# The tail of a GNN and mixture-of-experts layer: half of the experts' rows added on TensorE, small steps by pairs of loads, amplitude and base by diagonals

## The chip, the cores and the metric

The program runs on one core of a Trainium2 chip. The core has TensorE (PE, with its weight loads shown apart as PEld), VectorE (DVE), ScalarE (ACT), GpSimd (POOL) and SyncE (SP), which here only issues transfers, and 16 DMA engines. The metric is the device time of one execution in microseconds (us), given as the median of the runs.

## The reference, cut to what matters

A graph convolution with a residual, a top-2 mixture of 64 experts, a batch normalisation over the 12,500 nodes, then a sum with the input and a layer normalisation over the 256 columns. What the change touches is the end, from `y` on:

```python
    m = segment_sum(h[src], dst, n) * rsqrt(deg_in)[:, None]
    x = m @ W_gc + b_gc + (feats @ W_res + b_res)
    core = _moe_ff(x, Wg, bg, w1, b1, w2, b2)      # two experts a node, summed
    y = x + core
    mean = jnp.mean(y, axis=0)
    var = jnp.mean((y - mean) ** 2, axis=0)
    return (y - mean) * rsqrt(var + BN_EPS) * gamma + beta
...
x = _layernorm(x + gnn(x, ...), axis=-1)           # eps 1e-5
```

All of it is float32. Nodes are 12,500 rows, 256 columns.

## The kernel before

The program is one straight line of stages: the edges are ordered, the rows of the neighbours are gathered and summed on TensorE (the longest stage), the dense layers and the router follow, then the 64 experts, and last the tail, which begins at line 1400. A scheduler puts the instructions of each engine into an order when the program is built: by the order of the program, but an instruction that could start, by the scheduler's own reckoning, may go ahead of one that could not. On the chip each engine runs its list in that order. The SP list of transfers is such a list too: a transfer that waits for a buffer holds back those behind it.

The nodes are cut into 98 tiles of 128 (the last has 84), and the tail handles them in the 14 entries of `LOADS`: twelve of eight tiles (1 MB each), then tile 96 and tile 97 alone. The big buffer `acc` (`acc2` is its view in two halves of 128 columns) holds `x`, the residual stream, with nodes on the partitions; the experts have added their outputs to `z_d` in memory.

Pass 1 (L1417 to L1440) runs over `LOADS`. L1420 reads a load of `z_d` into `zt` (four buffers); L1422 adds it to `acc` on VectorE; L1433 turns each 128 x 128 block on TensorE with `ident`, four blocks to a PSUM buffer `q` of one bank (five buffers); L1438 takes the statistics of `q` on VectorE; L1440 copies `q` back over `acc` on ScalarE, so that columns are on the partitions afterwards. Then `fetch` (L1443 to L1447) reads the first five loads of the input `x` into the buffers `z` (pool `f_x`, five buffers).

Between the passes (L1452 to L1472) the statistics are merged and the two values per column, `amp` and `base`, are made. The helper `rsqrt` (L186 to L196) takes a square root on ScalarE, which has to load its table first, and four small steps on VectorE.

Pass 2 (L1473 to L1514) runs over `LOADS` again. L1478 scales each half of the load by `amp` and adds `base`, on ScalarE, in place. L1486 turns the blocks back on TensorE, four to a `q`; L1490 adds `q` to the input rows in `z` on VectorE; L1492 takes the statistics of each row. L1495 to L1508, with `rsqrt` among them, are the small steps, 13 on VectorE and a square root on ScalarE, over 8 columns at a time, which give each row's scale `rs` and shift `m`. L1510 applies them, one tile at a time, on ScalarE; L1513 stores the load, and L1514 fetches the load five further on into the buffer that this store frees.

Of the kernel before, what the change touches and what calls it, by code (L numbers as in the profile page):

```python
# [8 lines left out]
F32 = mybir.dt.float32  # L9
# [4 lines left out]
AF = mybir.ActivationFunctionType  # L14
ALU = mybir.AluOpType
# [4 lines left out]
P = 128  # L20
N = 12500
D = 256
# [3 lines left out]
EPS = 1e-5  # L26
# [70 lines left out]
LOADS = [(t, 8) for t in range(0, 96, 8)] + [(96, 1), (97, 1)]  # L97
# [4 lines left out]
def gnn_moe_kernel(  # L102
# [17 lines left out]
    nc = tc.nc  # L120
    V, S, T, GP = nc.vector, nc.scalar, nc.tensor, nc.gpsimd
# [10 lines left out]
    def rows(t):  # L132
        return P if t < NT - 1 else RAG
# [13 lines left out]
    ident = const.tile([P, P], F32)  # L147
# [7 lines left out]
    ones_f = const.tile([P, P], F32)  # L155
# [30 lines left out]
    def rsqrt(pool, o, d, tag=""):  # L186

        shape = [d.shape[0], d.shape[1]]
        r = pool.tile(shape, F32, name="rsq_r" + tag)
        S.activation(r, d, AF.Sqrt)  # L190
        V.reciprocal(r, r)
        q = pool.tile(shape, F32, name="rsq_q" + tag)
        V.tensor_mul(q, r, r)
        V.tensor_mul(q, q, d)
        V.tensor_scalar(q, q, -0.5, 1.5, op0=ALU.mult, op1=ALU.add)
        V.tensor_mul(o, r, q)  # L196
# [26 lines left out]
    acc2 = acc.rearrange("p (h n) -> p h n", h=2)  # L223
# [7 lines left out]
    bias = edge.tile([P, DL], F32)  # L231
# [21 lines left out]
    with ExitStack() as stack:  # L253
        one = stack.enter_context(tc.tile_pool(name="e_one", bufs=1))
        two = stack.enter_context(tc.tile_pool(name="e_two", bufs=2))
        ps1 = stack.enter_context(tc.tile_pool(name="e_ps1", bufs=1, space=PSUM))
        ps2 = stack.enter_context(tc.tile_pool(name="e_ps2", bufs=2, space=PSUM))
# [150 lines left out]
        for c0 in range(0, C0 + 1, CH):  # L408
            n = min(CH, C0 + 1 - c0)
# [143 lines left out]
    with ExitStack() as stack:  # L553
# [4 lines left out]
        for i, (t0, n) in enumerate(pieces):  # L558
            r = rows(t0)
# [74 lines left out]
    with ExitStack() as stack:  # L634
# [226 lines left out]
        def fetch(t0):  # L861
            if t0 >= NT:
                return
            n, r = (2, P) if t0 < NT - 2 else (1, rows(t0))
            xts[t0] = two.tile([P, 2, D], F32, name="xt", bufs=3)
            S.dma_start(xts[t0][:r, :n], x[t0 * P : t0 * P + (n - 1) * P + r].rearrange(
                "(t p) d -> p t d", p=r))
# [314 lines left out]
    with ExitStack() as stack:  # L1182
# [27 lines left out]
        at = 0  # L1210
# [189 lines left out]
    with ExitStack() as stack:  # L1400
        one = stack.enter_context(tc.tile_pool(name="f_one", bufs=1))
        two = stack.enter_context(tc.tile_pool(name="f_two", bufs=2))
        xq = stack.enter_context(tc.tile_pool(name="f_x", bufs=5))
        zq_stack = stack.enter_context(ExitStack())
        zq = zq_stack.enter_context(tc.tile_pool(name="f_z", bufs=4))
        ps1 = stack.enter_context(tc.tile_pool(name="f_ps1", bufs=1, space=PSUM))
        ps2 = stack.enter_context(tc.tile_pool(name="f_ps2", bufs=5, space=PSUM))

        gam = one.tile([P, 2], F32)
        nc.sync.dma_start(gam, gamma.rearrange("(h p) -> p h", p=P))  # L1410
        bet = one.tile([P, 2], F32)
        nc.sync.dma_start(bet, beta.rearrange("(h p) -> p h", p=P))


        stat = one.tile([P, 2, 25, 6], F32)
        z3 = z_d[:NP].rearrange("(t p) d -> p t d", p=P)
        for t0, n in LOADS:  # L1417
            r = rows(t0)
            zt = zq.tile([P, 8, D], F32, name="zt")
            nc.sync.dma_start(zt[:r, :n], z3[:r, t0 : t0 + n])  # L1420
            y = acc2[:r, :, t0 * P : (t0 + n) * P].rearrange("p h (t d) -> p t h d", d=P)
            V.tensor_add(y, y, zt[:r, :n].rearrange("p t (h d) -> p t h d", h=2))  # L1422
            if t0 == 96:
                continue
            for h in range(2):
                for b in range(0, n, 4) if t0 < 96 else [-1]:
                    q = ps2.tile([P, 4, P], F32, name="q")
                    at = 0
                    for i in range(4):
                        t = t0 + b + i  # L1430
                        if t < NT:
                            r = rows(t)
                            T.transpose(  # L1433
                                q[:, i, :r], acc2[:r, h, t * P : (t + 1) * P], ident[:r, :r]
                            )
                            at += r
                    q = q.rearrange("p a b -> p (a b)")[:, :at]
                    V.bn_stats(stat[:, h, (t0 + b) // 4], q)  # L1438

                    S.copy(acc2[:, h, (t0 + b) * P : (t0 + b) * P + at], q)  # L1440
        xt = {}

        def fetch(k):  # L1443
            if k < len(LOADS):
                t0, n = LOADS[k]
                xt[k] = xq.tile([P, 8, D], F32, name="z")
                nc.sync.dma_start(xt[k][: rows(t0), :n], part_of(x, t0, n))  # L1447

        for k in range(5):
            fetch(k)  # L1450

        mv = one.tile([P, 2, 2, 2], F32)  # L1452
        for h in range(2):
            V.bn_aggr(mv[:, h, 0], stat[:, h, :24])
            V.bn_aggr(mv[:, h, 1], stat[:, h, 24])

        full, rest = 24 * 512 / N, (N - 24 * 512) / N
        mean = one.tile([P, 2], F32)
        var = one.tile([P, 2], F32)
        gap = one.tile([P, 2], F32)  # L1460
        V.tensor_sub(gap, mv[:, :, 1, 0], mv[:, :, 0, 0])
        V.scalar_tensor_tensor(mean, gap, rest, mv[:, :, 0, 0], op0=ALU.mult, op1=ALU.add)
        V.tensor_mul(gap, gap, gap)
        V.tensor_scalar(var, mv[:, :, 0, 1], full, EPS, op0=ALU.mult, op1=ALU.add)
        V.scalar_tensor_tensor(var, mv[:, :, 1, 1], rest, var, op0=ALU.mult, op1=ALU.add)
        V.scalar_tensor_tensor(var, gap, full * rest, var, op0=ALU.mult, op1=ALU.add)
        amp = one.tile([P, 2], F32)
        rsqrt(one, amp, var, "_f")
        V.tensor_mul(amp, amp, gam)
        base = one.tile([P, 2], F32)  # L1470
        V.tensor_mul(base, mean, amp)
        V.tensor_sub(base, bet, base)  # L1472
        for g, (t0, n) in enumerate(LOADS):  # L1473
            r = rows(t0)
            z = xt[g][:r, :n]
            for h in range(2):
                y = acc2[:, h, t0 * P : (t0 + n - 1) * P + r]
                S.activation(y, y, AF.Identity, bias=base[:, h : h + 1], scale=amp[:, h : h + 1])  # L1478
            st = two.tile([P, 8, 6], F32, name="st")
            for i in range(0, n, 2):  # L1480
                k = min(2, n - i)
                q = ps2.tile([P, 4, P], F32, name="q")
                for j in range(k):
                    t = t0 + i + j
                    for h in range(2):
                        T.transpose(  # L1486
                            q[:r, 2 * j + h], acc2[:, h, t * P : t * P + r], ident
                        )
                zi = z[:, i : i + k].rearrange("p t d -> p (t d)")
                V.tensor_add(zi, q[:r, : 2 * k].rearrange("p a b -> p (a b)"), zi)  # L1490
                for j in range(k):
                    V.bn_stats(st[:r, i + j], z[:, i + j])  # L1492

            m = two.tile([P, 8], F32, name="m")
            V.tensor_add(m[:r, :n], st[:r, :n, 1], st[:r, :n, 4])  # L1495
            V.tensor_scalar_mul(m[:r, :n], m[:r, :n], -0.5)
            gap = two.tile([P, 8], F32, name="gap")
            V.tensor_sub(gap[:r, :n], st[:r, :n, 1], st[:r, :n, 4])
            V.tensor_mul(gap[:r, :n], gap[:r, :n], gap[:r, :n])
            ve = two.tile([P, 8], F32, name="ve")  # L1500
            V.tensor_add(ve[:r, :n], st[:r, :n, 2], st[:r, :n, 5])
            V.tensor_scalar(ve[:r, :n], ve[:r, :n], 1.0 / D, EPS, op0=ALU.mult, op1=ALU.add)
            V.scalar_tensor_tensor(
                ve[:r, :n], gap[:r, :n], 0.25, ve[:r, :n], op0=ALU.mult, op1=ALU.add
            )
            rs = two.tile([P, 8], F32, name="rs")
            rsqrt(two, rs[:r, :n], ve[:r, :n], "_t")
            V.tensor_mul(m[:r, :n], m[:r, :n], rs[:r, :n])  # L1508
            for i in range(n):
                S.activation(  # L1510
                    z[:, i], z[:, i], AF.Identity, bias=m[:r, i : i + 1], scale=rs[:r, i : i + 1]
                )
            nc.sync.dma_start(part_of(out, t0, n), z)  # L1513
            fetch(g + 5)  # L1514


# [39 lines left out]
```

## Time and profile before

| what | us |
|---|---|
| median of three runs (3351.6 to 3354.98) | 3354.48 |
| the profiled execution, whole | 3356.17 |
| the profiled execution, its span from first to last instruction | 3354.4 |
| last instruction of the experts on VectorE | about 3182 |
| first load of `z_d` issued by SP | 3189.83 |
| first add of pass 1 | 3195.62 |
| first scaling of pass 2 (L1478), right after `base` | 3258.64 |
| first store of the output issued | 3277.53 |
| last scaling of the output (L1510) begins | 3349.75 |

All times in the table but the first two count from the start of the span. Over the whole span the page gives PE 80% busy, VectorE 52%, ScalarE 25% and GpSimd 64%, but these are means over stages that have different limits; the tail is the last 172 us, and GpSimd has no work in it. A row of a group of instructions gives the line, the engine, the operation, the tile written and the tiles read, the shape, the number of instructions, then busy time and the mean of one in ns, then the idle time of that engine just before them and what ended it. The granted clock is that of TensorE, 1.00 being full speed.

### The profile page before, as it was taken

Reading aid. Unit: us, or ns where it says so; the run is one execution under the profiler, and the core shown is the slowest. Engines: PE = TensorE matmul, PEld = TensorE weight load, DVE = VectorE, ACT = ScalarE, POOL = GpSimd, SP = SyncE. Lnnn points to the kernel's source line nnn. Section 1 sums busy time; section 2 is a strip of 40 time slices with the busy share of each in tenths; the row PEclk is TensorE's granted clock in tenths of the full one; section 3 lists DMA queues with packets and bytes.
Section 4 is the critical chain, followed back from the end, with each engine's and each line's share of the span. In section 5 each row is a group of like instructions: output and inputs, shape, how many; then the busy total and the mean of one; then the engine's idle time right before and its main releaser. Section 6 shows DMA issues by size and latency. Waiting matters only on the chain. (4 is left out here: it accounts for less than half of the span.)

```text
span 3354.4 us, 37394 instructions
## 1 busy us (share of the span) xinstructions
PE 2688.7 (80%) x11121; PEld 1781.7 (53%) x11121; DVE 1738.0 (52%) x6714; ACT 828.1 (25%) x2097; POOL 2157.1 (64%) x2089
## 2 busy tenths in 40 slices
PE   6727787777887778787777877875999999999954
PEld 5613344444554445444444444553777776777843
DVE  9986334445545545544554454675333333333388
ACT  8960111111111111111111111121122211122258
POOL 0027777777777777777777777763777777777500
PEclk8856678988888887888888888887999999999975
DMA  9153444444444444444444444443556666777767
GB/s 349 57 163 105 151 120 125 125 123 128 126 125 127 124 129 121 127 127 126 121 130 125 126 127 126 128 119 94 118 128 141 142 143 157 169 185 193 172 217 243
DMA packets 258809, 476.57 MB, mean 142 GB/s; under 512 B 42689, under 2 KB 182941, under 8 KB 250281
## 3 DMA queue, kind: packets, MB, share of 16 engines
q0 software_dynamic: 119808, 268.62, 32.5%
q1 hardware_dynamic: 125494, 192.70, 17.7%
q10 hardware_dynamic: 13298, 12.80, 1.2%
q8 instruction: 91, 1.49, 0.2%
q14 instruction: 118, 0.96, 0.1%
HBM read 388.86 MB, written 85.10 MB: 141 GB/s over the span
## 5 line engine op out<-in xcount | busy, mean ns | idle before, releaser
L727 POOL DMA_INDIRECT ring<-h_d,src_col x1584 | 1524.5, 962 | 495.4 <-issue 429.7
L741 PE MATMUL p<-ring,o 128*128 128x258 f32 x3168 | 1204.4, 492 | 452.4 <-DMA ring<-h_d,src_col 362.6
L741 PEld LDWEIGHTS p<-ring,o 128*128 128x128 f32 x3168 | 623.8, 228 | 947.8 <-DMA ring<-h_d,src_col 621.2
L719 DVE TENSOR_SCALAR o<-lane,rel 128x128 f32<-128x128 f32 x1584 | 385.1, 302 | 615.2 <-PE p L741 615.2
L1302 POOL DMA_INDIRECT z_d<-yo,tables x241 | 376.1, 1561 | 115.5 <-issue 60.3
L1295 PE MATMUL yp<-w,h 128*128 128x256 f32 (+3 forms) x1928 | 433.1, 380 | 1.8 <-DVE yo L1300 1.8
L1269 PE MATMUL hp<-xT,w 128*128 128x384 f32 (+11 forms) x1328 | 399.5, 454 | 1.3 <-DVE xT L1260 1.3
L1295 PEld LDWEIGHTS yp<-w,h 128*128 128x128 f32 (+3 forms) x1928 | 341.2, 181 | 67.1 <-issue 7.3
L1241 POOL DMA_INDIRECT xg<-x_d,tables x241 | 236.4, 981 | 199.8 <-PE xtp L1256 97.4
L1273 ACT ACTIVATE h<-hp,w 128x384 f32<-128x384 f32 (+11 forms) x332 | 181.2, 546 | 671.7 <-PE hp L1269 670.9
L774 ACT COPY s<-p 128x258 f32<-128x258 f32 x132 | 49.4, 374 | 1134.0 <-PE p L741 1133.9
L1269 PEld LDWEIGHTS hp<-xT,w 128*128 128x128 f32 x1328 | 248.1, 191 | 131.6 <-issue 57.0
L1260 DVE COPY xT<-xtp 128x768 f32<-128x768 f32 (+2 forms) x83 | 77.4, 932 | 317.5 <-PE xtp L1256 317.5
L1300 DVE TENSOR_TENSOR yo<-yp,bb 128x256 f32<-128x256 f32 (+3 forms) x241 | 102.0, 423 | 209.7 <-PE yp L1295 199.6
L433 ACT ACTIVATE s_lo<-lane_b,nb 128x128 bf16<-128x128 bf16 x581 | 171.1, 386 | 4.7 <-DVE lo_end L424 2.1
L1057 PE MATMUL tab<-at,vals 128*128 128x512 bf16 x392 | 149.2, 473 | 14.6 <-DVE vals L1045 14.6
L581 POOL MEMSET acc<- 128x1792 f32 x10 | 17.5, 1748 | 214.0 <-DMA h_d<-acc 214.0
L839 DVE TENSOR_TENSOR acc<-q,acc 128x256 f32 x132 | 55.6, 421 | 154.7 <-PE q L816 122.6
L926 PE MATMUL bank<-wcat,acc 128*128 128x320 f32 x392 | 134.7, 470 | 0.0
L931 PE MATMUL bank<-wcat,xT 128*128 128x320 f32 x392 | 126.6, 447 | 0.0
L736 ACT CAST ring<-mark 128x4 f32<-128x4 bf16 x354 | 56.9, 193 | 250.0 <-issue 250.0
L926 PEld LDWEIGHTS bank<-wcat,acc 128*128 128x128 f32 x392 | 81.9, 210 | 31.8 <-issue 6.7
(278 smaller groups left out, 2779.5 us busy)
## 6 DMA issues: line engine op xcount, KB each, us to landing
w<-in_wpack SPq DMA_DIRECT2D x64, 1026.0 KB
ring<-h_d,src_col POOLq DMA_INDIRECT x1584, 2.8
tables<-h_d SPq DMA_DIRECT2D x118, 128.0 KB
z_d<-tables SPq DMA_DIRECT2D x53, 256.0 KB
x_d<-y SPq DMA_DIRECT2D x48, 258.0 KB
xt<-in_x ACTq DMA_DIRECT2D x48, 256.0 KB
zt<-z_d SPq DMA_DIRECT2D x12, 1024.0 KB
z<-in_x SPq DMA_DIRECT2D x12, 1024.0 KB
```

What stands on the lines that cost most here:

```text
L433: S.activation(s_lo[:, i], lane_b, AF.Sign, bias=nb[:, k, i : i + 1])
L719: o_last[u] = V.tensor_scalar(o_of[u][:, j], lane, rel[:, c : c + 1], None, op0=ALU.is_equal)
L727: i = GP.indirect_dma_start(out=r[:, k, :D], out_offset=None, in_=h_d, in_offset=bass.IndirectOffsetOnAxis(ap=src_col[:, c : c + 1], axis=0),)
L741: i = T.matmul(p_of[g], o_of[v][:, n], r[:, k], start=j == 0, stop=j == GR - 1)
L926: T.matmul(gps[i][:r], acc2[:, k, a : a + r], wcat[:, k], start=k == 0, stop=False,)
L931: T.matmul(gps[i][:r], v["xT"][:, i, k, :r], wcat[:, 2 + k], start=False, stop=k == 1,)
L1057: T.matmul(tab, vals[:r, m], at[:r], start=t0 + i + k + m == 0, stop=t0 + i == NT - 1 and k + m == 2,)
L1241: GP.indirect_dma_start(out=g, out_offset=None, in_=x2_d, in_offset=bass.IndirectOffsetOnAxis(ap=at[:, 0, k : k + 1], axis=0),)
L1269: T.matmul(hp[:, :m], w1[:, c, j * P : (j + 1) * P], xT[:, c, :m], start=c == 0, stop=c == 1,)
L1273: S.activation(h1[:, j, :m], hp[:, :m], AF.Gelu, bias=w[:, 2 * H + 4 * D + j : 2 * H + 4 * D + j + 1],)
L1295: T.matmul(yp[:r], h1[:, j, k * P : k * P + r], w2[:, j], start=j == 0, stop=j == 3,)
L1302: st = GP.indirect_dma_start(out=z_d, out_offset=bass.IndirectOffsetOnAxis(ap=at[:r, 1, k : k + 1], axis=0), in_=yo[:r], in_offset=None, c ...
```

## The change

In pass 1 the first load is read as two halves. Of each later load of eight tiles VectorE adds only the first four; for the other four TensorE turns the block of `acc` and, into the same place in PSUM, adds the turned block of `zt` by a matmul with `ident`. A square root of no use is placed before the pass, so that ScalarE's table is loaded there. The two loops over `h` and `b` change places.

In pass 2 the loads come in another order (the first, the two single tiles, then the rest), and in sets: the first alone, the others by twos, the last alone. The small steps are done once for a set, over up to 16 columns. Loads with an odd place in that order are treated as before. For the others L1478 is left out: TensorE multiplies each block by a diagonal of `amp` and adds a product of ones with a diagonal of `base`. The last load is stored in two halves. Six loads of the input are read ahead in place of five.

```diff
@@ pools
-        xq = stack.enter_context(tc.tile_pool(name="f_x", bufs=5))
+        xq = stack.enter_context(tc.tile_pool(name="f_x", bufs=6))
@@ pass 1
-        for t0, n in LOADS:
+
+        S.activation(stat[:, 0, 0, 0:1], ones_f[:, 0:1], AF.Sqrt)
+        for t0, n in [(0, 4), (4, 4)] + LOADS[1:]:
...
-            y = acc2[:r, :, t0 * P : (t0 + n) * P].rearrange("p h (t d) -> p t h d", d=P)
-            V.tensor_add(y, y, zt[:r, :n].rearrange("p t (h d) -> p t h d", h=2))
+
+            m = min(n, 4)
+            y = acc2[:r, :, t0 * P : (t0 + m) * P].rearrange("p h (t d) -> p t h d", d=P)
+            V.tensor_add(y, y, zt[:r, :m].rearrange("p t (h d) -> p t h d", h=2))
...
-            for h in range(2):
-                for b in range(0, n, 4) if t0 < 96 else [-1]:
+            for b in range(0, n, 4) if t0 < 96 else [-1]:
+                for h in range(2):
...
-                            T.transpose(
-                                q[:, i, :r], acc2[:r, h, t * P : (t + 1) * P], ident[:r, :r]
-                            )
+                            y = acc2[:r, h, t * P : (t + 1) * P]
+                            if b < 4:
+                                T.transpose(q[:, i, :r], y, ident[:r, :r])
+                            else:
+                                T.matmul(
+                                    q[:, i], y, ident, start=True, stop=False, is_transpose=True
+                                )
+                                T.matmul(
+                                    q[:, i], zt[:, b + i, h * P : (h + 1) * P], ident,
+                                    start=False, stop=True,
+                                )
...
+        order = LOADS[:1] + LOADS[12:] + LOADS[1:12]
+        sets = [[0], [1, 2], [3, 4], [5, 6], [7, 8], [9, 10], [11, 12], [13]]
...
-        for k in range(5):
+        for k in range(6):
             fetch(k)
@@ pass 2
-        for g, (t0, n) in enumerate(LOADS):
-            r = rows(t0)
-            z = xt[g][:r, :n]
-            for h in range(2):
-                y = acc2[:, h, t0 * P : (t0 + n - 1) * P + r]
-                S.activation(y, y, AF.Identity, bias=base[:, h : h + 1], scale=amp[:, h : h + 1])
-            st = two.tile([P, 8, 6], F32, name="st")
...
+        d_amp = one.tile([P, 2, P], F32)
+        d_base = one.tile([P, 2, P], F32)
+        for h in range(2):
+            V.tensor_scalar_mul(d_amp[:, h], ident, amp[:, h : h + 1])
+            V.tensor_scalar_mul(d_base[:, h], ident, base[:, h : h + 1])
+        for g, units in enumerate(sets):
+            st = two.tile([P, 16, 6], F32, name="st")
+            if g == 1:
+                V.memset(st, 0.0)
+            at = 0
+            for u in units:
+                t0, n = order[u]
...
+                by_act = u % 2
+                for h in range(2 * by_act):
+                    y = acc2[:, h, t0 * P : (t0 + n - 1) * P + r]
+                    S.activation(
+                        y, y, AF.Identity, bias=base[:, h : h + 1], scale=amp[:, h : h + 1]
+                    )
...
+                            to, y = q[:r, 2 * j + h], acc2[:, h, t * P : t * P + r]
+                            if by_act:
+                                T.transpose(to, y, ident)
+                            else:
+                                T.matmul(to, y, d_amp[:, h], start=True, stop=False)
+                                T.matmul(to, ones_f[:, :r], d_base[:, h], start=False, stop=True)
...
+            n = at
+            m = two.tile([P, 16], F32, name="m")
...
+            for u in units:
+                t0, n = order[u]
...
+                for i in range(n):
+                    S.activation(
+                        z[:, i], z[:, i], AF.Identity,
+                        bias=m[:r, at : at + 1], scale=rs[:r, at : at + 1],
+                    )
+                    at += 1
+
+                    if i == n - 1 or u == 13 and i == 3:
+                        b = 4 if u == 13 and i == n - 1 else 0
+                        nc.sync.dma_start(part_of(out, t0 + b, i + 1 - b), z[:, b : i + 1])
+                fetch(u + 6)
```

The small steps themselves, between `m` and the last loop, are those of before, now written for `n` columns of a set.

More of the change, by code (lines that the diff above doesn't have):

```diff
@@ L1440, in gnn_moe_kernel @@
                     S.copy(acc2[:, h, (t0 + b) * P : (t0 + b) * P + at], q)
+        order = LOADS[:1] + LOADS[12:] + LOADS[1:12]
+        sets = [[0], [1, 2], [3, 4], [5, 6], [7, 8], [9, 10], [11, 12], [13]]
         xt = {}
         def fetch(k):
-            if k < len(LOADS):
-                t0, n = LOADS[k]
+            if k < len(order):
+                t0, n = order[k]
                 xt[k] = xq.tile([P, 8, D], F32, name="z")
                 nc.sync.dma_start(xt[k][: rows(t0), :n], part_of(x, t0, n))
-        for k in range(5):
+        for k in range(6):
             fetch(k)
@@ L1472, in gnn_moe_kernel @@
         V.tensor_sub(base, bet, base)
-        for g, (t0, n) in enumerate(LOADS):
-            r = rows(t0)
-            z = xt[g][:r, :n]
-            for h in range(2):
-                y = acc2[:, h, t0 * P : (t0 + n - 1) * P + r]
-                S.activation(y, y, AF.Identity, bias=base[:, h : h + 1], scale=amp[:, h : h + 1])
-            st = two.tile([P, 8, 6], F32, name="st")
[L1480 to L1502, printed above, removed]
@@ new lines, in gnn_moe_kernel @@
+        d_amp = one.tile([P, 2, P], F32)
[10 more added lines that the diff above has]
+                t0, n = order[u]
+                r = rows(t0)
+                z = xt[u][:r, :n]
+                by_act = u % 2
[4 more added lines that the diff above has]
+                    )
+                for i in range(0, n, 2):
+                    k = min(2, n - i)
+                    q = ps2.tile([P, 4, P], F32, name="q")
+                    for j in range(k):
+                        t = t0 + i + j
+                        for h in range(2):
+                            to, y = q[:r, 2 * j + h], acc2[:, h, t * P : t * P + r]
[4 more added lines that the diff above has]
+                                T.matmul(to, ones_f[:, :r], d_base[:, h], start=False, stop=True)
+                    zi = z[:, i : i + k].rearrange("p t d -> p (t d)")
+                    V.tensor_add(zi, q[:r, : 2 * k].rearrange("p a b -> p (a b)"), zi)
+                    for j in range(k):
+                        V.bn_stats(st[:r, at + i + j], z[:, i + j])
+                at += n
+            n = at
+            m = two.tile([P, 16], F32, name="m")
+            V.tensor_add(m[:, :n], st[:, :n, 1], st[:, :n, 4])
+            V.tensor_scalar_mul(m[:, :n], m[:, :n], -0.5)
+            gap = two.tile([P, 16], F32, name="gap")
+            V.tensor_sub(gap[:, :n], st[:, :n, 1], st[:, :n, 4])
+            V.tensor_mul(gap[:, :n], gap[:, :n], gap[:, :n])
+            ve = two.tile([P, 16], F32, name="ve")
+            V.tensor_add(ve[:, :n], st[:, :n, 2], st[:, :n, 5])
+            V.tensor_scalar(ve[:, :n], ve[:, :n], 1.0 / D, EPS, op0=ALU.mult, op1=ALU.add)
@@ L1503, in gnn_moe_kernel @@
             V.scalar_tensor_tensor(
-                ve[:r, :n], gap[:r, :n], 0.25, ve[:r, :n], op0=ALU.mult, op1=ALU.add
+                ve[:, :n], gap[:, :n], 0.25, ve[:, :n], op0=ALU.mult, op1=ALU.add
             )
[L1506 to L1512, printed above, removed]
@@ L1513, in gnn_moe_kernel @@
-            nc.sync.dma_start(part_of(out, t0, n), z)
-            fetch(g + 5)
+            rs = two.tile([P, 16], F32, name="rs")
+            rsqrt(two, rs[:, :n], ve[:, :n], "_t")
+            V.tensor_mul(m[:, :n], m[:, :n], rs[:, :n])
+            at = 0
+            for u in units:
+                t0, n = order[u]
+                r = rows(t0)
+                z = xt[u][:r, :n]
+                for i in range(n):
[8 more added lines that the diff above has]
+                fetch(u + 6)
```

## The prediction

> **What bounds the tail now.** The page's chain of waits ends on the output scaling L1510 and says no more, so I cut the tail into stretches of time (stretch, length, busy us and instructions of PE, PEld, DVE, ACT, POOL, then granted clock, DMA share, GB/s):
>
> ```profile
> 3195.60:3256.00 60.40, 35.52 (x196) 33.38 (x196) 59.18 (x74) 29.24 (x51) 0.00 (x0) 0.73 0.86 276
> ...
> 3264.00:3327.00 63.00, 38.74 (x165) 29.33 (x163) 60.21 (x242) 57.22 (x100) 0.00 (x0) 0.55 0.71 232
> 3327.00:3355.00 28.00, 3.25 (x12) 2.08 (x12) 15.83 (x85) 16.47 (x37) 0.00 (x0) 0.50 0.62 206
> ```
>
> Pass 1 (add z, turn, statistics) is VectorE without a gap, 59.18 of 60.40 us. Pass 2 (normalise) is VectorE too, 60.21 of 63, ScalarE close behind at 57.22. TensorE has room, and the change gives it the work. The groups by line from 3000 to 3354 us say who waits:
>
> ```profile
> L1486 PE MATMUL q<-ident,acc 128*128 128x128 f32 x196 | 46.0, 405 | 33.7 <-DVE z L1490 24.6 <-ACT acc L1478 6.0 <-DVE rsq_q_t L193 0.9
> ...
> L1433 PE MATMUL q<-ident,acc 128*128 128x128 f32 x196 | 35.5, 362 | 37.0 <-DVE acc L1422 37.0
> ...
> L1490 DVE TENSOR_TENSOR z<-q,z 128x512 f32<-128x512 f32 (+2 forms) x50 | 32.4, 668 | 5.7 <-PE q L1486 3.5 <-DMA z<-in_x 2.2
> L1438 DVE BATCH_NORM_STATS2 stat<-q 128x6 f32<-128x512 f32 (+1 forms) x50 | 30.3, 668 | 0.4 <-PE q L1433 0.2
> L1478 ACT ACTIVATE acc<-acc,base,amp 128x1024 f32<-128x1024 f32 (+2 forms) x28 | 29.5, 1118 | 1.7 <-DVE base L1472 1.7
> ...
> L1422 DVE TENSOR_TENSOR acc<-acc,zt 128x2048 f32<-128x2048 f32 (+2 forms) x14 | 27.7, 2012 | 14.1 <-DMA zt<-z_d 14.1
> ```
>
> Both kinds of transpose wait for VectorE (37.0 and 24.6 us); VectorE waits for TensorE 0.2 and 3.5 us.
>
> **The price of a TensorE record** decides the case. A transpose is one record (196 = 98 tiles x 2 halves); an f32 matmul is two (L1269 and L1295 show twice the calls in the code). Single means overlap, so I use spacings in the timeline, (burst less its last record)/(count-1):
>
> ```profile
> 3143.55 0.60 PE L1256 MATMUL xtp<-ident,xg 128*128 128x128 f32 x4
> 3143.98 3.62 PE L1295 MATMUL yp<-w,h 128*128 128x256 f32 x16
> ...
> 3154.36 3.19 PE L1269 MATMUL hp<-xT,w 128*128 128x224 f32 x16
> ```
>
> At full clock a transpose takes 0.11 (3143.55 to 3143.98, four), a 256-column matmul record (3.62-0.38)/15 = 0.216, a 224-column one (3.19-0.35)/15 = 0.189: 0.00085 us a column. No 128-column f32 matmul is in the trace. By columns it would be 0.108; from the other side a 64-column one (L389, four in 0.62, last 0.275) is already at 0.115[...]. I take 0.115 for every record. At half clock eight transposes take 1.97, the last 0.45: 0.217 each, and I give matmuls the same. The clock is the question:
>
> ```profile
> 3198.00:3204.00 6.00, 6.00 (x32) 5.25 (x32) 5.42 (x7) 2.39 (x5) 0.00 (x0) 0.68 1.09 348
> ...
> 3226.70:3233.30 6.60, 6.50 (x32) 6.29 (x32) 6.35 (x8) 3.35 (x6) 0.00 (x0) 0.56 1.04 332
> ...
> 3294.00:3298.70 4.70, 3.74 (x15) 2.97 (x16) 3.98 (x13) 4.70 (x11) 0.00 (x0) 0.50 1.04 341
> ...
> 3110.00:3150.00 40.00, 40.00 (x202) 35.81 (x202) 14.88 (x41) 10.26 (x23) 20.19 (x15) 1.00 0.84 206
> ```
>
> Bursts of 32 transposes raise it to 0.56 to 0.72, pass 2's short bursts leave it at 0.50, continuous matmuls have 1.00. The gather stage, matmul records of 0.22 for 56% of the time (1578 records in 600 us), has 0.85. The Trainium skill speaks against the change: "TensorE: Matmul & The Clock Gate", Part 4, PE-mode transpose, says transposes don't count as activity and full clock doesn't engage for them. By that rule pass 1, where half the records stay transposes, might stay at 0.217: 372 records = 81 us. By the rows pure transposes do raise the clock, and the other half are matmuls: 372 x 0.115 = 43, or 46 at a clock near 0.9. I take 0.125 in all, because a TensorE that falls behind is continuously busy, which is where the rows show 1.00.
>
> **Pass 1, part by part.** VectorE adds only four tiles of eight. Two adds of 2048 take 4.47; the 256-wide takes 0.405, so 1024 wide is 1.2. Per load: 1.2 + 4 x 0.61 (eight statistics in 4.87) = 3.6 against 4.7. TensorE per load: 8 transposes alone, then 8 x (transpose + two matmul records) = 32 records instead of 16, 4.0 us at 0.125. DMA per load 1 MB at 340 GB/s = 3.1, plus fetches of x. So the bound moves to TensorE, 4.0 instead of 4.7. The split first load lets VectorE start when 0.5 MB has landed, about 1.5 us earlier (half of 3.1). Path: add ends 3195.3; 16 cold records, 3.5; load 1 is added at 3199.8; 356 records x 0.125 = 44.5 to 3244.3. From the last transpose to base was 3253.9 to 3258.6 = 4.7; the early Sqrt takes its table load off it (variance ready at 3256.08, Sqrt at 3256.76: 0.7; the skill's "ScalarE: Activation LUTs", What ACT_TABLE_LOAD costs, prices a switch at 2.66 with its drain, but here 0.6 of the 1.28 load was already hidden). Base at 3248.3 instead of 3258.6: -10.3. A buffer of z is now held until TensorE has read it, four are there (16 us of TensorE work against about 6 for a load to land), and ScalarE's copies, 0.59 x 4 per load, stay covered. I give back 1.3 for waits between three nearly equal resources: **-9.0**. Bounds: VectorE and DMA alone allow -13; a clock of 0.7 (0.159 a record) gives 0.
>
> **Pass 2.** Small steps: VectorE busied 75 us by groups, but in line two adds take 1.27 and four statistics 1.39, so 50 x 0.635 + 98 x 0.347 = 66; the rest of 3262.0 to 3340 less 2.2 of DMA waits is 10, over 14 sets 0.7 each. Fourteen sets become eight: -4.2. Twice as wide costs nothing that a row of 0.16 for 8 columns would show.
>
> Amplitude and base on TensorE: six loads of eight tiles, 16 blocks of four records, 64 records = 7.4 us warm, 8.0 at 0.125; the other six stay 16 transposes, 2. A pair is 10.0, VectorE's pair 2 x 5.3 + 0.7 = 11.3, five PSUM buffers even out the halves: covered, with 1.3 to spare. ScalarE per pair falls from 12.9 to 10.5 (two of four L1478 at 1.18 gone), so nothing waits there. Added ahead of TensorE: four diagonals of 0.24 (L797's 128x128). The first load meets a cold TensorE: 16 records x 0.217 = 3.5 for the first q, its add 4.5 after base (3.4 before), the next three q at 2.0, VectorE through at 11.8 with 5.3 of work: 6.5 of waits.
>
> VectorE's last statistics: work 66 + 7 sets x 0.7 = 70.9, + 6.5 = 77.4 after base. (The same sum for before, 66 + 13 x 0.7 + 3.4 + 2.2 = 80.7, stands beside 81.4 measured, 3258.6 to 3340.0.)
>
> DMA queue: six units are fetched ahead, but two are the single-tile ones, so 4.2 MB instead of 5.2. The seventh waits for the first output, 19 us after base as before; it is needed at about 33 and lands by 29. Later fetches sit on SP behind the output whose buffer they take, 8 us ahead of need by the same count. Then 4 MB per pair need 12.3 us at 340 GB/s against VectorE's 11.3, so slack shrinks by 1 us a pair: I charge +1: 78.4, against 81.4, **-3.0**.
>
> End: before, the span closes 14.4 after 3340.0, through ScalarE's backlog, three chains (8 columns, 1, 1) and the outputs. After, the single-tile units come early and the last set is one load stored in halves: ScalarE's 16 scalings of the pair before (8.1) end 4.6 after the last statistics, then 4.0 for the last eight, 0.5 MB (1.6, and 2.7 of latency, which the first z load took beyond its 3.1) and 0.5 to close: 13.4, **-1.0**. No fetch stands between these stores on SP.
>
> **Sum:** -9.0 - 3.0 - 1.0 = -13.0: the profiled run's 3356.2 (its span 3354.4 and 1.8 around it) becomes 3343.2; the median shown is 1.7 below that run, so **3341.5**.
>
> **Rivals.**
> 1. *The clock stays as it is* (0.72 in pass 1, 0.54 in pass 2): slower. Place: TensorE in both passes; price 0.156 and 0.20 a record; point of decision 0.159, a clock near 0.7. Pass 1 gains about 0; pass 2's 480 records take 96 us, with 2 at the ends 98 against 81.4, less 1 at the close: +16. **3370**. For: 0.50 in all of pass 2, the skill's rule. Against: 0.85 at 56% duty with matmuls.
> 2. *The order leaves bubbles*: VectorE's program order puts the next add behind the last statistics, so each pair of loads costs TensorE 0.7 + 1.2 + 0.1 = 2 us, 12 over six pairs: base at 3260.3, +1.7, less pass 2's 4: **3352**, no change. For: adds now come in twos, before eight statistics. Against: an add needs only its z.
> 3. *DMA takes over in pass 1*: if all x fetches precede the last z, 17.2 MB at 340 is 50.6, last z at 3243, 4.0 for its load and 4.0 to base, 3251: -7.5. **3343**. For: 340 GB/s already. Against: fetches stood between and behind the z loads before.
> 4. *It does not do what it says*: pairing only moves VectorE's steps to where it waits for ScalarE (57 of 63 us), and pass 1 alone gains: **3345.5**. Against: ScalarE loses 2.4 a pair.
>
> **From these to the numbers.** Main course 45%, rival 1 20%, rival 2 15%, rivals 3 and 4 together 20%. Its own range is 3333 to 3347. With 5% left below and half of rival 1 above: 3332 to 3362. About 0.2% (6.7 us, from 3347.8 to 3361.2) is what a measurement can tell from no change. Faster: 0.43 + 0.04 + 0.16 = 0.63; slower: 0.17 of rival 1 and 0.03 elsewhere = 0.20; the same 0.17.
>
> **What will show it.** Right: base near 3248, clock above 0.85 from 3200 to 3244, VectorE idle for TensorE (the releasers turn round) in pass 1 but busy in pass 2. Wrong: a clock under 0.7 with TensorE at full duty; a matmul record spaced over 0.16 at full clock; VectorE waiting for z in pass 2; first output later than 22 us after base.

## The result, and the profile after

The changed kernel takes 3339.47 us (median of six runs, 3338.4 to 3342.47), the one before, measured beside it, 3353.69 (3351.6 to 3355.25): 14.2 us less, a ratio of 0.9963 with a 95% interval of 0.9953 to 0.9973. The forecast was 3341.5.

The run profiled took 3339.96, its span is 3338.2. The stages ahead of the tail differ by some us from run to run, so the tail is measured by itself, from three points read in each trace, to about 0.1 us: the issue of the first load of `z_d`, the start of the first work that needs `base` (the last step between the passes), and the end of the last statistics of pass 2.

| profile | first z load to base | base to last statistics | from there to the end | sum |
|---|---|---|---|---|
| before | 68.8 | 81.4 | 14.4 | 164.6 |
| after | 57.9 | 76.7 | 16.1 | 150.6 |
| difference | -10.9 | -4.8 | +1.7 | -14.0 |

These are the stretches of the steady part of each pass, in the columns of the prediction's first fence:

```profile
3204.00:3235.00 31.00, 30.20 (x273) 29.87 (x271) 30.36 (x43) 19.38 (x33) 0.00 (x0) 1.00 1.01 319
3260.00:3312.00 52.00, 45.99 (x381) 42.52 (x381) 51.20 (x176) 32.89 (x69) 0.00 (x0) 1.00 0.87 287
```

TensorE is busy 30.20 of 31 us in pass 1 and 45.99 of 52 in pass 2, and its clock is 1.00 in both, where it was 0.73 and 0.55. (The traces also tell when the granted clock changes. It is 0.50 or 1.00 in all of them, never between, so a mean such as 0.73 is a share of the time at each.) VectorE is as full as before, 30.36 of 31 and 51.20 of 52. ScalarE has fallen in pass 2, from 57 of 63 to 33 of 52. The groups that answer to those of before, from 3180 to 3340 us:

```profile
L1523 DVE TENSOR_TENSOR z<-q,z 128x512 f32<-128x512 f32 (+2 forms) x50 | 32.5, 668 | 5.9 <-PE q L1521 5.8
L1444 PE MATMUL q<-ident,zt 128*128 128x128 f32 x176 | 31.5, 284 | 0.0
...
L1450 DVE BATCH_NORM_STATS2 stat<-q 128x6 f32<-128x512 f32 (+1 forms) x50 | 31.1, 673 | 2.9 <-PE q L1444 1.8 <-PE q L1439 0.9
...
L1426 DVE TENSOR_TENSOR acc<-acc,zt 128x1024 f32<-128x1024 f32 (+2 forms) x15 | 16.5, 1104 | 11.7 <-DMA zt<-z_d 11.7
...
L1507 ACT ACTIVATE acc<-acc,base,amp 128x1024 f32<-128x1024 f32 (+1 forms) x14 | 14.6, 1120 | 1.7 <-DVE base L1487 1.7
L1518 PE MATMUL q<-ident,acc 128*128 128x128 f32 x98 | 14.3, 279 | 5.1 <-DVE z L1523 4.9
```

The adds of z cost VectorE 16.5 us in place of 27.7 (L1426): the 11.2 that left are about pass 1's gain. The 176 matmul records that took their place (L1444) have no idle time before them. VectorE's longest waits in the tail (us in all, times, longest one):

```profile
DVE acc L1426 <- DMA zt<-z_d: 11.7, 2, 11.3
DVE rsq_r_t L191 <- ACT rsq_r_t L190: 6.1, 1, 6.1
DVE z L1523 <- PE q L1521: 5.8, 5, 3.3
DVE stat L1450 <- PE q L1444: 1.8, 3, 1.2
```

The first is the wait for the first load of z, there before too. The second is new: one wait of 6.1 us at the very end, for a square root. Of the third, 5.0 us are the cold TensorE at the start of pass 2: its clock is 0.50 until 5.5 us after `base`, with records spaced 0.213 us, and 1.00 from there on, with 0.112. The other 0.8, at an add 47.8 us after `base`, is not TensorE's, though the view puts it there: the `q` of that add had been ready for 5 us, and the add began 0.1 us after the last piece of its load of x had landed. In VectorE's timeline of pass 1 a load takes 3.53 us, without a gap:

```profile
3217.59 2.49 DVE L1450 BATCH_NORM_STATS2 stat<-q 128x6 f32<-128x512 f32 x4
3220.00 1.21 DVE L1426 TENSOR_TENSOR acc<-acc,zt 128x1024 f32<-128x1024 f32 x1
3221.13 2.49 DVE L1450 BATCH_NORM_STATS2 stat<-q 128x6 f32<-128x512 f32 x4
3223.53 1.21 DVE L1426 TENSOR_TENSOR acc<-acc,zt 128x1024 f32<-128x1024 f32 x1
```

From add to add, 3220.00 to 3223.53. It was 4.7.

### The profile page after: what moved, and what is told of

It reads as the page before. It is cut to its first block, busy times and chain, and to the rows that moved or that the text cites. A ratio compares the mean times of both kernels' runs of the same rounds, so it can differ in the third digit from the quotient of the medians.

```text
span 3338.2 us, 38239 instructions
## 1 busy us (share of the span) xinstructions
PE 2681.9 (80%) x11591; PEld 1787.0 (54%) x11591; DVE 1721.0 (52%) x6642; ACT 813.2 (24%) x2078; POOL 2152.6 (64%) x2089
## 5 line engine op out<-in xcount | busy, mean ns | idle before, releaser
L741 PE MATMUL p<-ring,o 128*128 128x258 f32 x3168 | 1183.2, 484 | 477.5 <-DMA ring<-h_d,src_col 391.5
L741 PEld LDWEIGHTS p<-ring,o 128*128 128x128 f32 x3168 | 608.1, 223 | 972.1 <-DMA ring<-h_d,src_col 638.9
L1057 PE MATMUL tab<-at,vals 128*128 128x512 bf16 x392 | 145.4, 462 | 15.2 <-DVE vals L1045 15.2
```

The source lines that it names most:

```text
L741: i = T.matmul(p_of[g], o_of[v][:, n], r[:, k], start=j == 0, stop=j == GR - 1)
L1057: T.matmul(tab, vals[:r, m], at[:r], start=t0 + i + k + m == 0, stop=t0 + i == NT - 1 and k + m == 2,)
```

## The experiments

Theory: pass 1 is worth what VectorE loses there, as TensorE takes the work at full clock; pass 2 gains by the pairs of small steps; the closing stretch grew because of ScalarE's order at the end. Rivals: transfers bound the tail; the diagonals carry pass 2.

The first eight kernels ran on two chips, four on each, on which the stages ahead of the tail take about 290 us longer (before: 3646 us on both). The tail itself is alike: on the first of the two, pass 1 of before took 68.8 us (p2_only), and pass 2 of before 81.9 and 14.3 (p1_only). So the three stretches are compared, and device times only with the runs of before beside them.

| kernel | first z load to base | base to last statistics | to the end | sum | device median, us (before beside it) |
|---|---|---|---|---|---|
| p1_only | 56.7 | 81.9 | 14.3 | 152.8 | 3634.9 (3646.3) |
| p2_only | 68.8 | 78.6 | 16.2 | 163.5 | 3644.3 (3646.3) |
| no_diag | 56.2 | 77.1 | 15.5 | 148.7 | 3629.4 (3646.3) |
| single_sets | 56.4 | 80.3 | 13.8 | 150.4 | 3630.3 (3646.3) |
| after_again | 56.8 | 75.9 | 16.1 | 148.7 | 3633.5 (3646.5) |
| split_end | 56.3 | 77.2 | 14.7 | 148.1 | 3627.3 (3646.5) |
| first_act | 59.2 | 76.0 | 16.2 | 151.3 | 3631.7 (3646.5) |
| pe_all | 73.2 | 80.0 | 16.1 | 169.4 | 3648.0 (3646.5) |
| vec_end | 57.9 | 79.8 | 10.6 | 148.2 | 3340.6 (3357.8) |
| vec_end_no_diag | 57.7 | 77.5 | 10.3 | 145.4 | 3338.5 (3357.8) |
| all_diag | 57.9 | 91.2 | 14.2 | 163.2 | 3355.9, one run (3357.8) |
| whole_first_late_sqrt | 57.6 | 78.5 | 16.2 | 152.2 | 3343.8, one run (3357.8) |

Each row of stretches is one profile. How far profiles of the same code scatter, and why, can be read in the traces.

In the first column nine of these kernels have the pass 1 of the changed kernel (all but p2_only, pe_all and whole_first_late_sqrt). Its length follows the moment, counted from the first load of z, at which TensorE's clock goes to 1.00 to stay: 9.2 to 9.5 us in the five at 56.2 to 56.8, 14.3 to 15.2 in the three at 57.7 to 57.9 (15.5 in the first profile of the changed kernel), 17.2 in first_act at 59.2. So the same code spans 3 us there, and a smaller difference says little unless the clocks are compared too.

In the second column five profiles have the pass 2 of the changed kernel, and they lie between 75.9 and 80.0. VectorE's work is the same in all five. Its waits for loads of x are not:

| profile | base to last statistics | VectorE busy in it | its waits for the first load's `q` | its waits for x |
|---|---|---|---|---|
| after | 76.7 | 70.7 | 5.0 | 0.8 |
| after_again | 75.9 | 70.7 | 4.1 | 0.9 |
| p2_only | 78.6 | 70.7 | 5.0 | 2.8 |
| whole_first_late_sqrt | 78.5 | 70.8 | 5.2 | 2.4 |
| pe_all | 80.0 | 70.8 | 4.2 | 5.0 |
| no_diag | 77.1 | 70.6 | 2.9 | 3.5 |
| first_act | 76.0 | 70.4 | 3.0 | 2.5 |
| single_sets | 80.3 | 75.6 | 4.5 | 0.0 |
| vec_end | 79.8 | 73.4 | 4.7 | 1.5 |
| vec_end_no_diag | 77.5 | 73.1 | 2.9 | 1.3 |
| p1_only (pass 2 of before) | 81.9 | 75.0 | 3.5 | 2.5 |

A wait is counted for x here when the add begins 0.1 us after its load of x has landed and its `q` had been ready for over 4 us; the view of waits puts some of these down to TensorE and some to nothing ("issue"). Why a load of x lands late in one profile and not in the next stays open. A total of the second column can thus be off by 4 us for that reason alone, and is read by its parts.

**p1_only and p2_only: each pass alone.** The files join pass 1 of the one kernel to pass 2 of the other; nothing else is edited.

> Pass 1 as in the changed kernel, pass 2 (and five x loads ahead) as before. Theory (the two passes add up, pass 1 is worth what VectorE loses as TensorE runs at full clock): from the first z load to base 57.8 us as after (68.7 before), base to the end as before (95.9): about 3343 us, 10.9 below before. Rival (the earlier start of pass 2 is given back, because the x loads and outputs then wait for transfers): base early all the same, but base to the end 100 us or more and the time at 3348 or above.

> Pass 1 as before (with its late square root table), pass 2 as in the changed kernel. Theory: first z load to base 68.7 us as before, base to the last statistics 76.7 and from there to the end 16.1 as after, so 92.8 instead of 95.9: about 3350.6, 3.1 below before. Rival (the pairs and diagonals of pass 2 carry the change, pass 1 is limited by transfers anyway): 3343 or less.

Pass 1 alone gains 12.1 in its stretch (56.7 for 68.8) and pass 2 then runs as before, 81.9 and 14.3. Nothing is given back: the rival falls, and the ratio is 0.9973 (0.9962 to 0.9983). Pass 2 alone gains 2.9, with 2.8 of waits for x in it where the changed kernel has 0.8, and gives 1.8 back at the end: 94.8 in all, where the theory had 92.8. Its ratio, 0.9997 (0.9988 to 1.0007), can't be told from 1. So pass 1 carries the change.

**no_diag: are the diagonals worth anything?**

```diff
-                by_act = u % 2
+                by_act = 1
```

> The changed kernel with every load scaled by ScalarE, no diagonals used. Theory (the diagonals pay because small steps by pairs make ScalarE the bound): ScalarE 12.9 us a pair against 11.3 of VectorE, 1.6 x 6 = 9.6 more, less about 2 because the first load no longer meets a cold TensorE: base to last statistics near 84 instead of 76.7, time 3346. Rival (ScalarE was never the bound, the diagonals are only cost): base to last statistics 74 to 75, time 3337.

Base to last statistics is 77.1, where after_again has 75.9, and the end is 0.6 shorter: the sums are equal, 148.7. The theory (84) is wrong. The rival (74 to 75) is missed by what x takes: no_diag waits 3.5 for x, after_again 0.9, and without that difference it would be at 74.5. The theory's mistake was to take ScalarE by the pair. ScalarE's timeline in no_diag:

```profile
3534.37 10.62 ACT L1507 ACTIVATE acc<-acc,base,amp 128x1024 f32<-128x1024 f32 x12 [1.74 <-DVE base L1487]
3544.91 0.19 ACT L190 ACTIVATE rsq_r_t<-ve 128x8 f32<-128x8 f32 x1
3545.00 2.36 ACT L1507 ACTIVATE acc<-acc,base,amp 128x1024 f32<-128x1024 f32 x2
```

It scales loads far ahead while it would otherwise wait for the first rows, and it may deliver the last ones after VectorE is through. Over the stretch it has 29.3 + 48.9 + 1.6 us of work (L1507, L1550, the roots), 79.8 of the 88.6 from base to the end of its last scaling, and between the first add and the last statistics VectorE never waits for it. So taking 14.7 us off it buys nothing. What the diagonals cost TensorE is hidden too, but for the start: there VectorE waits 2.9 without them, and 4.1 to 5.2 where the first load goes by diagonals. TensorE, with transposes alone, has a clock of 0.58 here (columns as in the prediction's first fence):

```profile
3537.00:3604.00 67.00, 44.43 (x192) 33.47 (x191) 64.34 (x222) 62.34 (x104) 0.00 (x0) 0.58 0.73 238
```

**single_sets: what are the pairs worth?**

```diff
-        sets = [[0], [1, 2], [3, 4], [5, 6], [7, 8], [9, 10], [11, 12], [13]]
+        sets = [[u] for u in range(14)]
...
-            if g == 1:
+            if g == 2:
```

> The changed kernel with the small steps done for each load alone, diagonals kept. Theory: six more sets at 0.7 us: base to the last statistics 80.9 instead of 76.7; but the last load's square root then stands behind 8 scalings of ScalarE, not 16, so from the last statistics to the end 12.5 instead of 16.1: 3340, the same within noise. Rival (pairs are worth more than their steps, as each set also interrupts VectorE's flow with a wait for the square root): base to last statistics 84 or more, time 3343 or more.

Base to last statistics is 80.3 against 75.9, 4.4 for six sets, 0.7 each as reckoned; by VectorE's busy time, 75.6 against 70.7, it is 0.8 each. The end is 13.8 against 16.1: the pairs give 2.3 of it back. The theory holds; of the 3.6 it expected at the end it got 2.3.

**after_again, split_end, first_act and pe_all** ran together.

> The changed kernel once more, beside the next three on one chip: first z load to base 57 to 58 us, base to the last statistics 76.7, then 16.1 to the end.

The changed kernel measures 56.8, 75.9 and 16.1 here, its device time 0.9961 of before (0.9947 to 0.9975).

```diff
-        sets = [[0], [1, 2], [3, 4], [5, 6], [7, 8], [9, 10], [11, 12], [13]]
+        sets = [[0], [1, 2], [3, 4], [5, 6], [7, 8], [9, 10], [11], [12], [13]]
```

> The changed kernel with the last pair of loads made into two sets of one. Theory (the closing stretch is long because the last set's square root stands on ScalarE behind the 16 scalings of the pair before): base to the last statistics +0.7, and 16.1 becomes about 12.5, as the root is behind 8: in all 3 us less than the changed kernel. Rival (the outputs' transfers set the end): the closing stretch stays at 15 or more and the time is 0 to 1 above the changed kernel.

The end shrank by 1.4, not 3.6, and the stretch before it grew by 1.3. The edit did not make what it was to make, as ScalarE's timeline shows:

```profile
3604.93 0.21 ACT L190 ACTIVATE rsq_r_t<-ve 128x8 f32<-128x8 f32 x1 [0.63 <-DVE ve L1538]
3606.90 7.97 ACT L1550 ACTIVATE z<-z,m,rs 128x256 f32<-128x256 f32 x16 [1.76 <-DVE rsq_q_t L194]
3614.77 0.20 ACT L190 ACTIVATE rsq_r_t<-ve 128x8 f32<-128x8 f32 x1
```

The first set's steps were so spread among VectorE's other work that both sets' scalings came in one row of 16 again, with the last root behind them. So this run tells nothing of the rival; vec_end was made for that.

```diff
-                by_act = u % 2
+                by_act = (u + 1) % 2
```

> The changed kernel with the roles exchanged: the loads at even places by ScalarE, those at odd places by diagonals, so the first load is only turned. Theory (VectorE's 5 us of waits at the start of pass 2 come from a cold TensorE with four records a block): waits 3 us or less, base to the last statistics 74 to 75. Rival (the cold records only move to the next load by diagonals): 76 to 77 as in the changed kernel.

76.0 against 75.9: the total is the rival's, but not for the rival's reason. VectorE's waits in pass 2:

```profile
DVE z L1523 <- PE q L1518: 3.0, 1, 3.0
...
DVE z L1523 <- PE q L1521: 1.4, 1, 1.4
DVE z L1523 <- DMA z<-in_x: 1.1, 1, 1.1
```

The 3.0 are at the start, as the theory says, 1.1 less than in after_again, and at the first load by diagonals VectorE does not wait at all. The 1.4 are at the last load, 70.3 us after base: its `q` had been ready for 6.4 us, and its x had landed 0.1 us before. So x takes 2.5 in place of 0.9, and that gives the gain back. (Pass 1, at 59.2, is code that was not touched; TensorE's clock rose late there.)

```diff
-            m = min(n, 4)
+            m = n if n < 8 else 0
...
-            V.tensor_add(y, y, zt[:r, :m].rearrange("p t (h d) -> p t h d", h=2))
+            if m:
+                V.tensor_add(y, y, zt[:r, :m].rearrange("p t (h d) -> p t h d", h=2))
...
-                            if b < 4:
+                            if n < 8:
```

> The changed kernel with all eight tiles of each 1 MB load added on TensorE, none on VectorE. Theory (a record costs 0.1105 us at full clock, and TensorE with 32 of them a load is level with VectorE at 3.53 us): 48 records are 5.3 a load, 11 x 1.77 = 19.5 more, first z load to base 77 us, VectorE waiting for TensorE, clock 1.00. Rival (VectorE alone sets pass 1 and TensorE has room): first z load to base 58 or less.

Now TensorE is the bound, and VectorE's timeline gives its price:

```profile
3512.30 0.70 DVE L1451 BATCH_NORM_STATS2 stat<-q 128x6 f32<-128x512 f32 x1 [0.63 <-PE q L1445]
3513.63 0.70 DVE L1451 BATCH_NORM_STATS2 stat<-q 128x6 f32<-128x512 f32 x1 [0.63 <-PE q L1445]
3514.96 0.70 DVE L1451 BATCH_NORM_STATS2 stat<-q 128x6 f32<-128x512 f32 x1 [0.63 <-PE q L1445]
```

One `q` each 1.33 us, 12 records: 0.111 a record, at clock 1.00. Pass 1 grew by 16.4, not 19.5. The 176 further records are 19.5 us of TensorE, so by this sum some 3 us of pass 1 are not TensorE's in the changed kernel: there it is level with VectorE. The device time is 1.0003 of before (0.9994 to 1.0013): half on each engine is the gain, all on TensorE loses it. Base to last statistics was 4.1 longer too, in code that was not touched. That is x: 5.0 of waits in place of 0.9. For the longest, 3.1, the view of waits names nothing that ended it; the add began 74.3 us after base, its `q` had been ready for 8 us, and its load of x, issued 67.9 after base, had landed 0.1 before.

**vec_end and vec_end_no_diag: the closing stretch.** Some of the last scalings go to VectorE, which has nothing else to do by then.

```diff
-                    S.activation(
-                        z[:, i], z[:, i], AF.Identity,
-                        bias=m[:r, at : at + 1], scale=rs[:r, at : at + 1],
-                    )
+                    if u == 12 or u == 13 and i % 2:
+                        V.tensor_scalar(
+                            z[:, i], z[:, i], rs[:r, at : at + 1], m[:r, at : at + 1],
+                            op0=ALU.mult, op1=ALU.add,
+                        )
+                    else:
+                        S.activation(
+                            z[:, i], z[:, i], AF.Identity,
+                            bias=m[:r, at : at + 1], scale=rs[:r, at : at + 1],
+                        )
```

> The changed kernel with the output scalings of the last load but one, and every second one of the last load, on VectorE. Theory (the closing stretch is ScalarE's: the last root waits behind 16 scalings, 6 us, and 8 more follow): only 8 stand before it and 4 follow; VectorE's eight scalings of 0.3 push the last statistics 2.5 later, from there to the end 8 instead of 16.1: from the first z load to the end 5 to 6 us less than the changed kernel (143 to 145), about 19 below before. Rival (the outputs' transfers set the end, as split_end moved it by little): 1 us less or none, 14 below before.

> The same with every load scaled by ScalarE, no diagonals used. Theory (the diagonals are neither gain nor cost, as ScalarE has room over the whole stretch and runs its scalings ahead): the same as vec_end within 1.5 us from the first z load to the end. Rival (the diagonals pay once the end no longer hides ScalarE's lateness): 3 us or more behind vec_end.

ScalarE's end in the changed kernel, and then in vec_end:

```profile
3320.84 7.96 ACT L1550 ACTIVATE z<-z,m,rs 128x256 f32<-128x256 f32 x16 [3.05 <-issue]
3328.71 0.19 ACT L190 ACTIVATE rsq_r_t<-ve 128x8 f32<-128x8 f32 x1
3330.23 4.04 ACT L1550 ACTIVATE z<-z,m,rs 128x256 f32<-128x256 f32 x8 [1.33 <-issue]
```

```profile
3324.41 4.04 ACT L1556 ACTIVATE z<-z,m,rs 128x256 f32<-128x256 f32 x8 [3.46 <-DVE m L1543]
3329.05 0.21 ACT L190 ACTIVATE rsq_r_t<-ve 128x8 f32<-128x8 f32 x1 [0.61 <-DVE ve L1538]
3330.60 2.07 ACT L1556 ACTIVATE z<-z,m,rs 128x256 f32<-128x256 f32 x4 [1.33 <-DVE m L1543]
```

With 16 scalings before it the root (L190) ran 6.6 after the last statistics (3322.1); with 8 it waits only for its own input, 0.8 after them (3328.2). The end falls from 16.1 to 10.6, so it is ScalarE's row and not the transfers. But VectorE's eight scalings took 2.67, and the stretch before grew by 3.1: the sum gains 2.4 on the first profile of the changed kernel and 0.5 on after_again, not 5 to 6. Without the diagonals it is 145.4, 2.8 less than vec_end and 5.2 less than after (3.3 less than after_again). The theory allowed 1.5 between the two. Of the 2.8, 1.8 are at the start of pass 2, where VectorE waits 2.9 without the diagonals and 4.7 with them, as no_diag and first_act show too. So the diagonals cost 1 to 2 us at the start and gain nowhere. By device time vec_end is 0.9951 of before (0.9937 to 0.9964) and vec_end_no_diag 0.9943 (0.9928 to 0.9959). The intervals overlap with the changed kernel's: faster by the profile's stretches, not separated by the runs.

**all_diag and whole_first_late_sqrt.** The first has `by_act = 0`; the second is:

```diff
-        S.activation(stat[:, 0, 0, 0:1], ones_f[:, 0:1], AF.Sqrt)
-        for t0, n in [(0, 4), (4, 4)] + LOADS[1:]:
+        for t0, n in LOADS:
```

> The changed kernel with diagonals for all loads. Theory (a record costs 0.1105 at full clock): a load is 64 records, 7.1 us, against VectorE's 5.7, twelve loads 85 us, so TensorE is the bound: base to last statistics 90 instead of 76, VectorE waiting for it. Rival (at full clock TensorE still keeps up, as its room is larger than the sum says): 78 or less.

91.2, as the price says: TensorE is the bound, and VectorE waits for it 29 times, 11.7 us in all. Six loads of twelve were under the limit, twelve are over.

> The changed kernel without the early square root and with the first z load whole. Theory: the first add comes 1.4 to 1.6 us later after the first z load's issue (5.8 instead of 4.35), and the merged variance waits 0.7 more for its root: first z load to base 2 more than the changed kernel. Rival (a later start is absorbed, as TensorE and VectorE then catch up on loads that have landed): 1 or less.

57.6, against 57.7 to 57.9 in the three kernels that ran beside it. The rival, 1 or less, holds; that nothing is lost is not shown, as TensorE's clock was at 1.00 here from 12.4 us after the first load on, and in those three only from 14.3 to 15.2. By the profiles with an earlier clock (56.2 to 56.8 at 9.2 to 9.5 us) up to 1 us may be lost. VectorE's timeline at its start:

```profile
3195.62 1.23 DVE L1425 TENSOR_TENSOR acc<-acc,zt 128x1024 f32<-128x1024 f32 x1 [12.88 <-DMA zt<-z_d]
3198.06 0.70 DVE L1449 BATCH_NORM_STATS2 stat<-q 128x6 f32<-128x512 f32 x1 [1.21 <-PE q L1438]
3198.67 1.21 DVE L1425 TENSOR_TENSOR acc<-acc,zt 128x1024 f32<-128x1024 f32 x1
```

The first add begins 5.8 us after the first issue (3189.8), 1.5 later than in the changed kernel (3187.6 to 3192.0). But the second load of 1 MB is added 8.9 after it, here, and 9.7 in the changed kernel, each time 0.2 to 0.3 us after it has landed: from the second load on nothing is late. The late table load cost 0.2, since this time it ran beside the merging of the statistics.

## Why the prediction was right, and where it was not

The forecast was a gain of 13.0; the profiles show 14.0, the runs 14.2. By its steps:

- **The price of a record.** Taken as 0.115 at full clock and 0.125 in all. It is 0.111 at full clock (12 in 1.33 us, pe_all), the same for a turn and a matmul record, as assumed, and 0.119 in all (the 356 records from the second load of pass 1 on took 42.3 us).
- **The clock.** The step that decided, and it was right: 1.00 in the steady part of both passes. The rule of the Trainium skill that the prediction set against it ("TensorE: Matmul & The Clock Gate", Part 4, PE-mode transpose) holds here only in part. Pure transposes do raise the clock, in spells: in pass 1 of before it goes between 0.50 and 1.00, 0.73 in the mean. But they do not hold it: no_diag's pass 2, of transposes alone, has 0.58. Whether it is the matmul records or the fuller engine that holds it is not shown, since both changed together (TensorE busy 66% of the time in no_diag's pass 2, 88% and 97% in the two passes of the changed kernel). The first rival, at 3370, needed 0.7. Its break-even price, 0.159 a record, comes out of the prediction's own sum as 0.150 to 0.154.
- **Pass 1**, -9.0 forecast, -10.9 measured (-12.1 in p1_only, whose clock rose earlier). The load takes 3.53 in place of 4.0, and the sum without the 1.3 given back for waits stood at -10.3. Pass 1 did not become TensorE's alone: VectorE stayed as full as before, where the prediction had it waiting. The bubbles of the second rival are not there: from the third load to the tenth each add stands before the last one or two statistics of the load ahead of it. Nor did transfers take over, as the third rival had it: after the first load VectorE waits 0.4 for z.
- **The first load in halves and the early root** brought 1 us at most (whole_first_late_sqrt), where the sum counted 1.5 and 0.7. A start 1.5 earlier is worth little when the second load has only just landed.
- **Pass 2**, -3.0 forecast, -4.8 measured. The pairs are as reckoned (0.7 to 0.8 a set), and VectorE's work too (70.7 for 70.9). The cold start was set at 6.5 of waits and took 5.0: that is most of the difference. The charge of 1 for transfers came to 0.8 in that profile, but to 2.8 and 5.0 in others with the same pass 2, so here the forecast was also lucky. The fourth rival, that pairing only moves VectorE's steps into waits for ScalarE, falls: between the first add and the last statistics there is no such wait. But about half of what the pairs gain there, 4.4, is given back at the end, 2.3 (single_sets).
- **Diagonals.** Rightly taken as hidden by VectorE; that they gain nothing was not seen, as ScalarE was read as close to the bound from its busy share in the steady part.
- **The end**, -1.0 forecast, +1.7 measured: the one step of the wrong sign. It said that the 16 scalings end 4.6 after the last statistics and the last eight follow at once. They ended 6.6 after, and the last set's own root and its six steps, 1.5 more, stood behind them in ScalarE's order. single_sets (13.8) and vec_end (10.6) show that this is the cause.

So two gains were taken too low by 1.9 and 1.8, and one loss was read as a gain of 1.0. That the sum came out only 1.0 off is in part luck: the errors, 3.7 and 2.7, stood against each other. Not tried alone were the exchange of the two loops in pass 1, and the order of the loads and the sixth buffer of x in pass 2.

## What to carry to other kernels

When work moves to an engine that waits, its price must be taken at the clock it will have with the new work, not at the one it has while idling: price the instruction by spacings at both clocks, and ask which of the two a full engine would be granted. Of the three shares measured here, none, half and all, half was the best, and there both engines took the same time per load; all of it on the new engine gave the whole gain back. And an engine with a busy share of 90% in the steady part need not be a bound: count its work against the whole stretch in which it may run ahead or late. Batching small steps saves their fixed cost once a batch and pays at the end, where the last batch stands behind the output work of the one before. And when two versions differ by a few us, look for a wait that neither was to change: here the loads of x moved the second stretch by 4 us under the same code.

## What the runs showed of the hardware that was not expected

- Transposes and f32 matmul records of 128 columns cost the same, 0.111 us at clock 1.00 (after, pe_all): what a product with a diagonal costs over a turn is its number of records.
- The same pass 1 had TensorE at clock 1.00 for good from 9.2 us after the first load in one profile (after_again) and from 17.2 in another (first_act), and took 56.8 and 59.2 us. Between the passes of the changed kernel the clock fell to 0.50, from 3244.1 to 3251.0; then it stayed at 1.00 from there to 3315.8, with TensorE idle for 12% of 3260 to 3312.
- VectorE's scaling of 128 x 256 f32 with a factor and a term for each partition took 0.33 each (eight in 2.67, vec_end), a third less than ScalarE's 0.50. Even so it pays only in time that VectorE has to spare: the stretch in which it did eight of them grew by 3.1.
